# A graph network's setup rearranged: where the adjacency flags go, when signs are checked, which engine takes the first norms, and when later weights load

## The chip, the cores and the metric

The kernel runs on one core of a Trainium2 chip. The time is that of one execution on the device, in microseconds. Lower is better. Three executions of the kernel before took 4068.27, 4077.92 and 4077.22 us; their median is 4077.22 us.

The core has five instruction queues that work beside each other: TensorE (PE in the profile; its weight loads are listed apart as PEld), VectorE (DVE), ScalarE (ACT), GpSimd (POOL) and SyncE (SP), which here issues nearly all DMAs. Each queue runs its instructions in the order in which they stand in the program and waits on semaphores for the others.

## What is computed

The input is x, 16 graphs of 1024 nodes with 256 features each, and one adjacency matrix adj of 1024 x 1024 integers, shared by all graphs. Four layers follow, each of the form

```
h = max(layernorm(x), 0)
x = x + layer(h, adj)
```

Layers 0, 1 and 2 are graph attention: q = h W, a score for each pair of nodes from two dot products (leaky ReLU of their sum), masked where adj is not positive, a softmax over the neighbours, and the weighted sum of q, then ELU (layers 0 and 2) or ReLU (layer 1). Layer 0 has four heads of 64 features, layers 1 and 2 have one of 256. Layer 3 is a transformer block with eight heads of 32: queries, keys and values, scores masked by adj > 0, softmax, weighted sum, a residual with a layer norm, a feed-forward of two 256 x 256 products and another residual with a layer norm. All is in float32.

## The kernel before

`direct` computes everything with exponentials that are not shifted by their maximum, and at the end makes a flag that says whether that was safe; only if not, a slower function (`general`) runs after it. Part of the safety check is that adj has no negative entry: `least` holds the minimum of each row of adj.

**Tiling.** A graph's x is two half tiles `xh` of 128 partitions x 4 x 256 (1024 nodes are 8 blocks of 128). The mask is one tile of bytes, 128 x 8 x 1024, adj transposed, made once and kept. `w_aug[l]` holds the weights W of graph layer l with three columns per head added, which give the two dot products.

**Setup** (`setup`). `prepare(l)` loads W and the vector a of layer l, and VectorE multiplies and sums them into the added columns (L585, L596, L606, L614). `neighbours(it)`, for each of the eight row blocks of adj, loads 512 KB into a tile of the ring `pa` (L623); VectorE turns it into flags 0 or 1 in a second tile of `pa` (L628); TensorE transposes them (L531), ScalarE casts the result to bytes in the mask (L646), and VectorE takes the minimum of the integers (L655). The ring `pa` has six tiles, so that three blocks of adj can be in work at once. Then come the weights of layer 3.

**The start of a graph** (`begin`). x[b] is loaded in two halves (L1600); ScalarE sums each block (L1610) and its squared deviations (`spread_of`, L444 and L448); in `gat`, VectorE and GpSimd turn these into 1/standard deviation (`inverse_of_squares`, L460 and L468), and ScalarE applies the norm (`normal`, L502).

**A graph layer** (`gat`). TensorE transposes the normed blocks and multiplies them with `w_aug` (L772); ScalarE takes exponentials of the added columns (L783). The row side of the exponentials is transposed, written to DRAM (`turn_rows`, L845) and read back to all partitions (`spread`, L854) as `row`. VectorE makes the masked attention weights `pt` from `row`, a column and the mask (`weights`, L870). Layer 0 multiplies them in four column groups of TensorE (L984, and L994 for the sums), layers 1 and 2 in full form (L897).

**Layer 3** (`attention`). Queries and keys are projected (L1134), split into two parts `hi` and `lo` whose sum is exact, written to DRAM (`hl`, L1152) and copied back into the stacks `ks` and `qs` (L1158), so that one matmul (L1355) gives a score of full precision. ScalarE takes the exponential (L1379), VectorE applies the mask (L1388), and TensorE multiplies with the values in four column groups (L1220). `feed` does the feed-forward; its `back` loads x again in four parts (L1505) and stores the result (L1577).

**What sets the order.** Nothing of this is emitted where it stands in the code. Each step is recorded with its engine, an estimated duration, what it reads and writes, and a key; a key comes from a base (the graph's number) and a curve over the layer's steps (`KNOTS`). `Record.schedule` then plays the steps forward with these durations, gives each engine the ready step of the lowest key, and emits them in that order. `PASS` is the delay that it counts from an engine's end to a reader on another engine, `SLACK` the same for DMAs; `moved` and `lands` are a DMA's time on the engines and to its landing; `LEAD` moves ScalarE's and VectorE's keys forward; `BIAS` weighs TensorE's cost of changing between its forms (`SWITCH`). So a changed constant can move any instruction of the kernel. Buffers are rings: a new use waits for the last readers of the old one. While graph 0 is in layer 0, graph 1 goes through layer 0 beside it with buffers lent by layer 3 (`lent`).

Of the kernel before, what the change touches and what calls it, by code (L numbers as in the profile page):

```python
# [22 lines left out]
P = 128  # L23
# [93 lines left out]
PASS = {"pe": 0.122, "act": 0.556, "dve": 0.232, "pool": 0.13, "dma": 0.0}  # L117
# [26 lines left out]
class Record:  # L144
# [138 lines left out]
SLACK = 0.722  # L283
KNOTS = {
    "gat0": (-10.926, -10.742, -7.218, -4.626, -2.628, -2.099, -0.444, -3.636, -2.816),
    "gat1": (0.191, 0.25, 0.454, 0.45, 0.566, 0.582, 0.633, 1.016, 0.672),
    "gat2": (1.126, -0.076, -0.221, -0.062, 0.894, -0.428, 0.959, 1.018, 1.17),
    "beside": (1.093, 3.374, 4.836, 2.176, 5.971),
    "values": (1.444, -1.53, -3.682, -3.253, 0.902, 0.891, 2.874, 0.851, 0.421),
    "steps": (0.98, 1.188, 1.323, 1.512, 1.578, 1.712, 2.006, 2.02, 1.489),  # L290
    "feed": (2.026, 2.163, 1.768, 1.658, 2.343, 1.828, 2.009, 2.223, 3.042),
    "last": (3.521, -0.495, 0.103, 1.329, 1.339, 5.969, 5.585, 3.41, 5.439),
}
BIAS = 2.241
LEAD = {"act": 8.212, "dve": 0.635}
# [33 lines left out]
def direct(ctx, tc, flag, x, adj, gat_w, gat_a, w_qkv, ln1_g, ln1_b, ln2_g, ln2_b, w1, b1, w2, b2, out):  # L329
# [219 lines left out]
    b_aug = [Buf(t, []) for t in w_aug]  # L549
    b_mask, b_least, b_qkv, b_feed = (Buf(t, []) for t in (mask, least, wqkv_sb, w1_sb))  # L550

    def prepare(l):
# [11 lines left out]
            [],  # L564
# [11 lines left out]
            [],  # L576
# [42 lines left out]
    def neighbours(it):  # L619
        a32, nat = r_pa.new(), r_pa.new()  # L620
# [4 lines left out]
        nat_f = nat.t.rearrange("p a n -> p (a n)")  # L625
        dve(
            ts_us(N),
            lambda: nc.vector.tensor_scalar(nat_f, a_i, 0.0, None, ALU.is_gt),  # L628
            [nat],
            [a32],  # L630
        )
        for j0 in range(0, NT, TH):
# [9 lines left out]
                [nat],  # L642
# [10 lines left out]
        dve(  # L653
            tt_us(N),
            lambda: nc.vector.tensor_reduce(least[:, it : it + 1], a_i, AX.X, ALU.min),  # L655
            [b_least(it)],
            [a32],
        )

    def mask_of(hf):  # L660
        return [b_mask((it, j0)) for it in range(hf * TH, (hf + 1) * TH) for j0 in (0, TH)]

    def setup():
        rec.stream(-3.0, (0.0, 1.0), False)
        prepare(0)
        rec.stream(-0.9, (0.0, 0.1), False)
        for it in range(NT):
            neighbours(it)
# [8 lines left out]
            [],  # L677
# [10 lines left out]
        dma(5.0, 2.5, load_feed, [b_feed], [], us=5.7)  # L688
# [38 lines left out]
    def gat(xt, b_mv, b_rstd, l, my):  # L727
# [8 lines left out]
        for hf in range(2):  # L736
# [3 lines left out]
            inv = inverse_of_squares if l in SQUARED else inverse  # L740
# [107 lines left out]
        def spread(hf, h, rd):  # L848

            row = my.row.new()  # L850
            dma(
                1.2,
                2.07,
                lambda: nc.sync.dma_start(  # L854
                    row.t,
                    rd.t[h * TH : (h + 1) * TH, :]
                    .rearrange("t n -> (t n)")
                    .partition_broadcast(P),
                ),
                [row],  # L860
                [rd],
            )
            return row
# [220 lines left out]
    def attention(b, xt, b_mv, b_rstd):  # L1084
# [42 lines left out]
        def project(g, hf, keys, stack, at):  # L1127
# [23 lines left out]
            for k, part in enumerate((hi, lo)):  # L1151
                dma(0.65, 1.5, lambda: nc.sync.dma_start(hl.t[:, k, :], part.t), [hl(k)], [part])  # L1152
            for a in range(4):
                k = ((0, 0, 1, 1), (0, 1, 0, 1))[keys][a]
                dma(
                    1.0,
                    1.83,
# [77 lines left out]
        for n in range(len(steps) + LAG):  # L1235
            m = n - LAG
            if m >= 0:
# [13 lines left out]
                elif jt % run:  # L1251
                    for ss, pt in zip(sums[g, hf], pas[m]):
                        dma(
                            2.8,
                            0.85,
# [145 lines left out]
    def feed(b, x3, hn):  # L1401
# [95 lines left out]
        def back(hf):  # L1497
            yT = yTs[hf]
            for it in (hf * TH, hf * TH + 2):
# [3 lines left out]
                    1.0,  # L1503
                    1.83,
# [86 lines left out]
    def begin(b):  # L1591
        xt, b_mv, b_rstd = Halves(r_xh), r_mv.new(), r_rstd.new()
        x_b = x[b].rearrange("(t p) c -> p t c", p=P)
        rec.stream(b, (0.0, 0.0), False)
        for hf in range(2):
# [6 lines left out]
                [],  # L1602
                b - 1.0,
            )
        for hf in range(2):
            its = range(hf * TH, (hf + 1) * TH)
            for it in its:
# [18 lines left out]
    def graph(b, state, l, my=own, knots=None):  # L1626
        rec.stream(b, knots or KNOTS[f"gat{l}"])
        gat(*state, l, my)
# [17 lines left out]
    states = [begin(0), begin(1)]  # L1646
    graph(0, states[0], 0)
    borrowed = lent()
    graph(0, states[1], 0, borrowed, KNOTS["beside"])
    for r in vars(borrowed).values():  # L1650
        if isinstance(r, Lent):
            r.give_back()
    for b in range(NB):
# [617 lines left out]
```

## Time and profile before

| | us |
|---|---|
| median of three executions | 4077.22 |
| the profiled execution, whole | 4072.03 |
| its span (first to last instruction) | 4070.3 |
| busy: TensorE | 4012.3 |
| busy: VectorE | 3501.7 |
| busy: ScalarE | 2666.6 |
| busy: GpSimd | 621.0 |

A busy TensorE is not TensorE at its peak: matmuls overlap, and their ends are modelled. The profile also has the clock that was granted to TensorE: 0.50 to 1.00 in the first 60 us, 1.00 nearly all the time after that. In the rows of the profile, the arrow in brackets names what ended the idle time before an instruction. The chain of waits follows the work back from the last instruction: at each step to what released it, or to the instruction before it on its engine.

### The profile page before, as it was taken

To read this page: it belongs to the slowest core of one execution; us is meant where nothing else is said; L and a number is where in the kernel's file an instruction comes from. 1 tells how busy PE (TensorE), PEld (TensorE's weight loads), DVE (VectorE), ACT (ScalarE), POOL (GpSimd) and SP (SyncE) were. 2 spreads that over 40 slices of the span, in tenths; PEclk is the share of its full clock that TensorE was granted. 3 is DMA by queue.
4 is the path that set the end of the run, shared out by engine and by line. 5 is a ranking of instruction groups with operands and counts; after the bars stand their busy time and mean duration, and the time that the engine had idled before them with its cause. 6 is when DMAs were issued, how large, how long until landed. Compare 5 with 4: busy or idle time off the path is not lost.

```text
span 4070.3 us, 66071 instructions
## 1 busy us (share of the span) xinstructions
PE 4012.3 (99%) x23874; PEld 2352.0 (58%) x23874; DVE 3501.7 (86%) x5994; ACT 2666.6 (66%) x6673; POOL 621.0 (15%) x631
## 2 busy tenths in 40 slices
PE   7999999999999999999999999999999999999998
PEld 4566466564655646566564665646556465665643
DVE  7778898989989899898988989899898998989866
ACT  5467575775757767576675766757577675766765
POOL 1101111111111112111111111111111121111200
PEclk9999999999999999999999999999999999999999
DMA  3034454444545345463444544445543454624451
GB/s 128 27 103 115 126 126 109 113 104 115 124 125 123 83 117 126 115 150 76 126 110 123 127 110 113 104 115 122 127 121 82 117 128 115 150 69 121 112 137 51
DMA packets 227520, 456.54 MB, mean 112 GB/s; under 512 B 24688, under 2 KB 59760, under 8 KB 227184
## 3 DMA queue, kind: packets, MB, share of 16 engines
q1 hardware_dynamic: 192624, 326.39, 28.3%
q0 software_dynamic: 34560, 125.84, 16.2%
q8 instruction: 190, 3.11, 0.3%
q14 instruction: 146, 1.20, 0.1%
HBM read 225.25 MB, written 101.06 MB: 80 GB/s over the span
## 4 chain that ended last, share of the span: by engine, by line
PE 94%; DMA 3%; ACT 1%; DVE 1%; issue 0%; SPq 0%; DVEq 0%; ACTq 0%; POOLq 0%
PE bank L897 21%; PE bank L1220 16%; PE sc L1355 12%; PE bank L984 11%; PE bank L772 9%; PE bank L531 6%; PE sc L1134 5%; PE bank L1452 5%; PE bank L994 5%; PE sc L1172 3%; DMA sums<-pa 2%; PE sc L531 1%; DVE pt L870 1%; ACT waste L448 0%; ACT pa L1379 0%
## 5 line engine op out<-in xcount | busy, mean ns | idle before, releaser
L1388 DVE TENSOR_TENSOR pa<-pa,mask 128x1024 f32<-128x1024 f32 x1024 | 1222.7, 1219 | 166.1 <-ACT pa L1379 162.6
L1379 ACT ACTIVATE pa<-sc 128x512 f32<-128x512 f32 x2048 | 1101.6, 611 | 370.1 <-DVE sums L1247 174.4
L870 DVE SCALAR_TENSOR_TENSOR pt<-row,e,mask 128x512 f32<-128x512 f32 x1472 | 1011.9, 744 | 46.6 <-DMA row<-rd 27.7
L897 PE MATMUL bank<-qb,pt 128*128 128x257 f32 x4096 | 941.0, 380 | 0.0
L897 PEld LDWEIGHTS bank<-qb,pt 128*128 128x128 f32 x4096 | 770.6, 190 | 143.6 <-issue 20.1
L1355 PE MATMUL sc<-qs,ks 128*128 128x512 f32 x2048 | 727.9, 457 | 2.6 <-DMA hl<-hi 1.1
L1220 PE MATMUL bank<-pa,va 128*32 128x512 f32 x4096 | 515.0, 597 | 0.0
L1355 PEld LDWEIGHTS sc<-qs,ks 128*128 128x128 f32 x2048 | 361.3, 189 | 237.9 <-ACT pa L1379 82.5
L984 PE MATMUL bank<-pt,qb 128*32 128x512 f32 x3840 | 461.7, 596 | 6.5 <-DVE pt L870 6.5
L1247 DVE TENSOR_TENSOR sums<-pa,pa 128x1024 f32<-128x1024 f32 x360 | 434.1, 1220 | 16.7 <-PE bank L1220 14.2
L772 PE MATMUL bank<-w_aug,hT 128*128 128x259 f32 (+1 forms) x1504 | 373.3, 389 | 0.0
L1256 POOL DMA_DIRECT2D sums<-pa x240 | 211.5, 883 | 954.1 <-DVE pa L1388 426.6
L772 PEld LDWEIGHTS bank<-w_aug,hT 128*128 128x128 f32 x1504 | 280.3, 190 | 99.6 <-ACT qb L794 35.4
L925 ACT ACTIVATE ex<-bank,rec 128x256 f32<-128x256 f32 x256 | 121.4, 475 | 288.9 <-DVE rec L917 288.7
L984 PEld LDWEIGHTS bank<-pt,qb 128*32 128x32 f32 x3840 | 116.5, 110 | 294.8 <-issue 219.5
L1220 PEld LDWEIGHTS bank<-pa,va 128*32 128x32 f32 x4096 | 115.0, 109 | 250.6 <-issue 225.7
L994 PE MATMUL bank<-pt,e 128*32 128x512 f32 x1920 | 252.0, 593 | 0.1
L1134 PE MATMUL sc<-hTa,wqkv_sb 128*128 128x512 f32 x512 | 240.0, 596 | 0.0
L468 POOL TENSOR_TENSOR rstd<-rstd,neg_half 128x4 f32<-128x4 f32 x96 | 169.2, 1762 | 362.1 <-DVE rstd L460 362.0
L1143 ACT CAST hi<-sc 128x512 fp32r<-128x512 f32 x128 | 75.1, 587 | 211.8 <-PE sc L1134 122.0
L502 ACT ACTIVATE hn<-xh,mv,rstd 128x256 f32<-128x256 f32 x376 | 202.8, 613 | 7.5 <-DVE mv L492 4.1
L1220 PE MATMUL bank<-sums,ones 128*32 128x512 f32 x1440 | 200.5, 600 | 3.9 <-DMA sums<-pa 3.7
(152 smaller groups left out, 4501.0 us busy)
## 6 DMA issues: line engine op xcount, KB each, us to landing
sums<-pa POOLq DMA_DIRECT2D x240, 512.0 KB, 6.0
ks<-hl SPq DMA_DIRECT2D x256, 256.0 KB
qs<-hl SPq DMA_DIRECT2D x256, 256.0 KB
row<-rd SPq DMA_DIRECT2D x184, 256.0 KB
hl<-hi SPq DMA_DIRECT2D x128, 256.0 KB
hl<-lo SPq DMA_DIRECT2D x128, 256.0 KB
xh<-in_x_dram SPq DMA_DIRECT2D x32, 512.0 KB
x<-xh SPq DMA_DIRECT2D x32, 512.0 KB
```

The costliest lines, as they stand in the source:

```text
L531: nc.tensor.transpose(dst(k), src(k), ident[:shape, :shape])
L772: nc.tensor.matmul(g.t[:, : C + 3 * H], hT.t[:, ct, k * P : (k + 1) * P], w_aug[l][:, ct, :], start=ct == 0, stop=ct == CT - 1,)
L870: lambda: nc.vector.scalar_tensor_tensor(pt.t, row.t, e3[:, 2, jt // TH, h, jt % TH : jt % TH + 1], mask[:, jt, hf * HALF : (hf + 1) * HAL ...
L897: nc.tensor.matmul(g.t[:, : D + 1], pts[jt].t[:, k * P : (k + 1) * P], qb[:, jt, 0, :], start=jt == 0, stop=jt == NT - 1,)
L984: nc.tensor.matmul(g.t[u * D + d : u * D + d + D3, :], qb[:, j, h + u, d : d + D3], pts[u][j - jt].t, start=j == 0, stop=j == NT - 1,)
L994: nc.tensor.matmul(gd.t[c : c + D3, :], one(jt + k, h + u).to_broadcast([P, D3]), pts[u][k].t, start=jt == 0, stop=jt == NT - 2,)
L1134: nc.tensor.matmul(sc.t, wqkv_sb[:, ct, c0 : c0 + P], hT.t[:, ct, hf * HALF : (hf + 1) * HALF], start=ct == 0, stop=ct == CT - 1,)
L1220: nc.tensor.matmul(ac.t[r * D3 : (r + 1) * D3, :], columns(r), of_head(r), start=first, stop=last,)
L1247: lambda: nc.vector.tensor_add(ss.t, p0.t, p1.t),
L1355: nc.tensor.matmul(scs[r - r0].t, ks.t[:, r, jt * P : (jt + 1) * P].bitcast(F32R), q.t[:, r, :].bitcast(F32R), start=True, stop=True,)
L1379: lambda: nc.scalar.activation(pt.t[:, v, :], sc.t, AF.Exp, scale=1.0 / math.sqrt(D3)),
L1388: lambda: nc.vector.tensor_mul(pt.t, pt.t, mask[:, jt : jt + 1, i0 : i0 + HALF].to_broadcast([P, 2, HALF]),),
```

## The change

Five things are edited.

1. The flags of the adjacency blocks go into the key stack `ks`, which nothing uses before layer 3, and no longer into tiles of `pa`. It has four parts of 128 x 1024, so that four blocks of flags are in work, and up to six loads of adj.
2. The minimum for the sign check is taken out of `neighbours`. A new function `signs`, recorded after graph 0's and graph 1's layer 0, loads adj a second time into the two tiles `yT` of the feed-forward and takes the minimum there.
3. Graph 0's first norm takes mean and variance from VectorE (`stats`: bn_stats and bn_aggr, L437 and L438, then `inverse`, L480 and L492), where ScalarE made sums and squares. The other graphs stay as they were.
4. Later loads are made to wait for the reads of the first rows in `spread`: x of graph 1 for the second, x of graph 2 and the weights of graph layers 1 and 2 for the fourth, the weights of layer 3 for the eighth. These are waits for the row's landing (`AFTER_ROWS`), ahead of the load on SP's queue.
5. The planner's constants: `PASS`, `SLACK`, `KNOTS`, `BIAS`, `LEAD`, and `moved` and `lands` of several DMAs have new values.

```diff
-PASS = {"pe": 0.122, "act": 0.556, "dve": 0.232, "pool": 0.13, "dma": 0.0}
+PASS = {"pe": 0.05, "act": 0.5, "dve": 0.263, "pool": 0.13, "dma": 0.0}
...
-SLACK = 0.722
+SLACK = 0.71
 KNOTS = {
...
-BIAS = 2.241
-LEAD = {"act": 8.212, "dve": 0.635}
+BIAS = 1.386
+LEAD = {"act": 10.373, "dve": 1.021}
...
+    rows_out = Buf(None, [])
+    n_rows = [0]
+    AFTER_ROWS = [[rows_out(n)] for n in range(8)]
...
 prepare(l): loads of w_aug and a
-            [],
+            AFTER_ROWS[3] * (l > 0),
...
-    def neighbours(it):
-        a32, nat = r_pa.new(), r_pa.new()
+    def neighbours(it, nat):
+        a32, part = r_pa.new(), nat(it % HG)
...
-        nat_f = nat.t.rearrange("p a n -> p (a n)")
+        nat_f = nat.t[:, it % HG, :]
         dve(
             ts_us(N),
-            lambda: nc.vector.tensor_scalar(nat_f, a_i, 0.0, None, ALU.is_gt),
-            [nat],
+            lambda: nc.vector.tensor_scalar(nat_f.bitcast(F32R), a_i, 0.0, None, ALU.is_gt),
+            [part],
...
-        dve(
-            tt_us(N),
-            lambda: nc.vector.tensor_reduce(least[:, it : it + 1], a_i, AX.X, ALU.min),
-            [b_least(it)],
-            [a32],
-        )
+
+    def signs():
+        rec.stream(0, (0.9, 1.6), False)
+        for it in range(NT):
+            again = r_yT.new()
+            a_i = again.t.rearrange("p a n -> p (a n)").bitcast(I32)
+            dma(1.8, 1.7, lambda: nc.sync.dma_start(a_i, adj[it * P : (it + 1) * P, :]), [again], [])
+            dve(
+                tt_us(N),
+                lambda: nc.vector.tensor_reduce(least[:, it : it + 1], a_i, AX.X, ALU.min),
+                [b_least(it)],
+                [again],
+            )
...
 setup
+        nat = r_ks.new()
         for it in range(NT):
-            neighbours(it)
+            neighbours(it, nat)
+
+    def setup_later():
         rec.stream(-0.5, (0.0, 0.3), False)
         prepare(1)
         prepare(2)
 loads of w_qkv and of the feed-forward's weights
-            [],
+            AFTER_ROWS[7],
...
 spread
-                1.2,
-                2.07,
+                1.45,
+                1.75,
...
-                [row],
+                [row] + [rows_out(n_rows[0])] * (n_rows[0] < 8),
                 [rd],
             )
+            n_rows[0] += 1
...
 begin
-        rec.stream(b, (0.0, 0.0), False)
+        rec.stream(b, (0.0, 0.0) if b else (-5.0, -5.0), False)
...
-                [],
+                AFTER_ROWS[1 if b == 1 else 3] * (b in (1, 2)),
                 b - 1.0,
             )
         for hf in range(2):
             its = range(hf * TH, (hf + 1) * TH)
+            if b == 0:
+                for it in its:
+                    stats(xt.at(it), xt(it), b_mv.t[:, 0, it, :], b_mv((0, it)))
+                continue
...
     setup()
-    states = [begin(0), begin(1)]
-    graph(0, states[0], 0)
+    states = [begin(0)]
+    graph(0, states[0], 0, first=True)
+    setup_later()
+    states.append(begin(1))
     borrowed = lent()
     graph(0, states[1], 0, borrowed, KNOTS["beside"])
     for r in vars(borrowed).values():
         if isinstance(r, Lent):
             r.give_back()
+    signs()
```

## The prediction

> **What bounds the kernel now.** I read the page first (span, busy shares, chain), then the first 60 us in windows of 20 us, the order of time in that stretch, the chain of waits row by row, and last the stretch where TensorE stops near the end.
>
> ```profile
> span 4070.3 us, 66071 instructions
> PE 4012.3 (99%) x23874; PEld 2352.0 (58%) x23874; DVE 3501.7 (86%) x5994; ACT 2666.6 (66%) x6673; POOL 621.0 (15%) x631
> ...
> PE 94%; DMA 3%; ACT 1%; DVE 1%; issue 0%; SPq 0%; DVEq 0%; ACTq 0%; POOLq 0%
> ```
>
> TensorE is the bound: only 58 us of the span are free of it. A change can win those 58 us, the stretches in which TensorE runs slowly, or the cost of changing between its instruction forms; elsewhere nothing.
>
> ```profile
> 0.00:20.00 20.00, 4.78 (x25) 4.32 (x26) 12.84 (x35) 13.02 (x39) 1.89 (x8) 0.96 0.86 313
> 20.00:40.00 20.00, 16.45 (x90) 14.36 (x89) 15.34 (x37) 15.46 (x48) 1.58 (x3) 0.84 0.77 229
> 40.00:60.00 20.00, 14.92 (x100) 5.34 (x100) 12.19 (x25) 17.92 (x62) 4.91 (x4) 0.77 0.09 28
> 60.00:80.00 20.00, 19.60 (x150) 9.56 (x147) 18.38 (x34) 7.52 (x17) 0.75 (x1) 1.00 0.10 27
> 80.00:100.00 20.00, 19.61 (x158) 7.67 (x160) 19.96 (x43) 6.09 (x15) 2.91 (x2) 1.00 0.19 55
> ```
>
> Columns: window, length, busy us of PE, PEld, DVE, ACT, POOL, clock, DMA share, GB/s. TensorE idles 15.2 + 3.6 + 5.1 = 24 us in the first 60. From 60 on it is full, but VectorE is as full (18.4 and 20.0 of 20). At 40 to 60 ScalarE is the full one (17.9).
>
> ```profile
> 10.50 0.69 DVE L628 TENSOR_SCALAR pa<-pa 128x1024 f32<-128x1024 int32 x1 [1.91 <-DMA pa<-in_adj_dram]
> 30.23 0.34 SPq L845 DMA_DIRECT2D rd<-rt  x1
> 34.41 0.82 SPq L854 DMA_DIRECT2D row<-rd  x2
> 43.14 0.17 DVE L460 TENSOR_SCALAR rstd<-mv 128x4 f32<-128x4 f32 x1 [5.35 <-ACT waste L448]
> 43.21 5.38 DVE L870 SCALAR_TENSOR_TENSOR pt<-row,e,mask 128x512 f32<-128x512 f32 x8
> 44.10 4.01 PE L984 MATMUL bank<-pt,qb 128*32 128x512 f32 x14 [6.51 <-DVE pt L870]
> 51.99 0.17 DVE L460 TENSOR_SCALAR rstd<-mv 128x4 f32<-128x4 f32 x1 [1.86 <-ACT waste L448]
> ```
>
> The first weights (L870) start at 43.2: VectorE stands 5.35 us in an L460 that needs batch 1's squares (L448) from ScalarE, which is busy with batches 1 and 2. It stands there again at 52. The row write took 4.2 us from its issue at 30.23 to the row read at 34.41, while other loads kept the DMA engines 0.77 to 0.86 busy.
>
> **Setup.** Removed from ScalarE: batch 0's eight sums (0.54 us a step at L1610), eight squares (0.64 at L448) and two L444 (0.2): 9.8 us. Added to VectorE: eight bn_stats and bn_aggr; four pairs took 1.6 us at 83.5 to 85.8 in the trace, so 3.3. Removed from early VectorE: eight sign reductions of 1.21 (L655), 9.7 us. In the new order eight bn_stats stand ahead of the first flags, so the first flags come not at 10.5 but at: x lands 7.7 (first L1610), plus 3.3, plus the w_aug work between (1.6) = about 12.9. TensorE so starts at 13.6 where it started at 11.3, which costs 2.3. After that the flags need no buffer turn-round: six adjacency loads are out at once instead of three, and the flags have the key stack's four places to themselves. The two x half loads come first as before. ScalarE does four norms (0.52) from 12.2, four mask casts (0.6), two copies, four norms, four casts: to 24. The projections (four of 0.9) follow their banks to 26, their second half to about 32; the first row write goes at 28.5 and, with the other loads held back, its read at about 31 (2.2 instead of 4.2 us). First weights at about 35, first L984 at about 36 instead of 44.1: **-8**. The L460 waits after it (TensorE's slow stretch from 44 to 52, about 5 us beyond its matmuls at later rates) go, because batch 1's x is asked for only after the second row, and its L460 stands behind sixteen weights (10.6 us): **-5**. What is late next is VectorE: the w_aug work for layers 1 and 2 (16 of 0.42, 8 of 0.16: 8 us; before it stood in VectorE's waits) now falls among the weights at 60 to 115 us, where VectorE has no room but TensorE has layer 1's matmuls soon after. Between 0 and 8 of it reach TensorE; I take **+5**, since 80 to 100 is 19.96 of 20. Setup -8, bounds -13 and 0. On F32R flags no row of VectorE exists: 0.69 each (L628) if nothing changes, 1.21 (the full-rate L655) if it does, so 0 to 4.2 us; I take 0, the row nearest in operation.
>
> The granted clock belongs here: 0.50 at 20 to 25 and 40 to 45, each after TensorE had idled (16.0 to 19.8, 37.6 to 44.1); 16 L531 took 3.66 us early against 0.89 for 8 later. The Trainium skill (TensorE: Matmul & The Clock Gate, Part 1) says that an idle window of about 3.4 us halves the clock and that one busy window restores it. By that rule a start without such gaps would regain about 5 us of half-speed work. I count none of it by itself; most of it is inside the 5 above.
>
> **Held loads on SP's queue.** x of batch 1 waits for row 2's landing, x of batch 2 and w_aug for row 4, w_qkv and the feed weights for row 8. Behind them stand the next row reads, which wait for a free row buffer anyway (two buffers; SP waited 73 times for L870 weights). Cost 0; if that cover went, a landing of 3 us each time, three times, in a DVE-full stretch: +9 at most.
>
> **Signs later.** Eight 512 KB loads into two tiles and eight 1.21 reductions move to the turn from batch 0's graphs to its attention. VectorE has room there: 7.8 of 20 busy at 160 to 180, 22.4 of 50 at 200 to 250. But six loads wait on SP for the reduction before, with hl, ks and qs behind. A 256 KB reload took 2.85 us in the chain, so a turn is about 4 us; all six on the path would be +24, none 0. The planner put two or three between projections whose results are needed at once; I take **+3**.
>
> **The order of everything else.** The planner's constants and curves change, so TensorE's order changes all along; its instructions do not. What an order costs is read from the chain:
>
> ```profile
> 114.25 0.86 PE bank L994 x8
> 115.11 1.02 PE bank L531 x8
> 116.14 1.85 PE bank L984 x16
> 117.99 0.86 PE bank L994 x8
> 118.85 1.95 PE bank L772 x8
> ```
>
> Eight L772 take 1.82 after their own kind and 1.95 here, sixteen L984 1.72 and 1.85: a turn into four-column form (L984, L994, L1220) and out again costs 0.26. A visit to the scores (L1355) from full form costs about 0.06: in the order of time four scores start at 1013.00 and the next form at 1014.01, 1.01 us, where four take 0.92 in the chain at 3918; four L531 ahead of them start at 1012.59 and last 0.41 instead of 0.44. Counted in the two built orders, column visits fall from 413 to 397, score visits from 736 to 667: 16 x 0.26 + 69 x 0.06 = **-8**. Bounds -2 (score visits free, half the column price) and -12 (direction of each change priced apart).
>
> **The last batch.** No later batch fills TensorE there:
>
> ```profile
> 3892.30 0.39 SPq L1577 DMA_DIRECT2D out_dram<-xr  x1
> 3897.55 0.32 SPq L1505 DMA_DIRECT2D xr<-x  x1
> 3897.99 0.39 SPq L1577 DMA_DIRECT2D out_dram<-xr  x1
> 3901.47 0.32 SPq L1505 DMA_DIRECT2D xr<-x  x1
> 3901.89 1.81 SPq L1158 DMA_DIRECT2D qs<-hl  x4
> ```
>
> The first queries' copies stand behind two stores and two reloads until 3901.9, though their data was written at 3891.5; scores start at 3911.2, and TensorE loses about 14 us by 3920. In the new order these copies stand ahead of the stores; only the second half of the keys, wanted four steps later, is behind one. The copies go 8 us sooner: **-8**, bounds -12 and 0 (norms at L502 hold TensorE 4.9 us in the same place).
>
> **Sum.** -8 +3 -8 -8 = -21. Against the profiled execution's own 4072.0 (span 4070.3): 4051. The median of the runs shown is 4077.2, from 4068.3 to 4077.9; the profiled one lies in the lower half, so I put 2 on it: 4053. Under 0.3% (12.2 us on 4077.2) this kernel's runs can't tell a change.
>
> **Rivals.**
> 1. Gains swallowed, 0.2. VectorE is the real bound to 115 us: the w_aug work costs all 8, flags at 1.21 add 4: setup 0. Switches -2, last batch -4, signs +3: 4069, within 0.3%. For it: 19.96 of 20. Against it: layer 1's matmuls need little VectorE (7.8 of 20 at 160). That the start is not sooner at all is this case.
> 2. Slower, 0.12. The planner now counts 0.05 us from TensorE to a reader (was 0.122) and 0.5 from ScalarE (was 0.556). Queues run in their written order, so if the old figures were the true ones, each of 1,024 score pairs can wait for its bank. At 0.05 a pair: +51, 4102. It decides from 0.035 a pair (36 us: the 21 and 12 more, with the profile's 3 to 5 below the median). Against it: TensorE waits for L1379 at the scores only 0.7 us in all now.
> 3. Better than forecast, 0.08: setup -13, switches -12, last batch -12, signs 0: 4035.
>
> The forecast has 0.6; its own range is 4038 to 4064. The range of all, 4036 to 4086, leaves out rival 2's bulk and the end of rival 3. Faster: 0.6 + 0.08 + a little of rival 1 = 0.71; same 0.17; slower 0.12.
>
> **What would show it.** Right: first L984 at 34 to 38; no L460 waiting 5 us for L448; clock 1.00 from 26 on; DVE over 19 of 20 through 110; no TensorE gap over 3 us in the last batch's first scores; PE busy below 4000. Wrong: first L984 after 42; SP waiting in L667 with PE idle at 215 to 330; PE rows at L1378 idling behind L1402; a new gap where the last batch's second keys are read.

## The result and the profile after

The kernel after took 4060.06 us (median of 7 runs, 4056.57 to 4066.36), the kernel before 4072.20 us beside it (7 runs, 4068.26 to 4077.92). The ratio is 0.9971, 95% interval 0.996 to 0.9982: faster by 12 us, just at the 0.3% that the prediction took as the limit of what can be told. 4053 was predicted, 4036 to 4086 as the range; 0.71 was put on faster.

The page of the kernel after, its first lines and the shares of the chain of waits:

```profile
span 4064.5 us, 65781 instructions
PE 4005.3 (99%) x23874; PEld 2354.6 (58%) x23874; DVE 3495.1 (86%) x6010; ACT 2691.8 (66%) x6639; POOL 640.0 (16%) x631
...
PE 80%; DMA 6%; ACT 5%; DVE 4%; issue 3%; POOL 1%; SPq 0%; POOLq 0%; DVEq 0%; ACTq 0%
```

The profiled execution of the kernel after (4066.36 us, the longest of its seven) is 5.7 us shorter than that of before; which stages are shorter still in the median run no profile shows. TensorE is busy 7.0 us less and idle 1.2 us more (59.2 for 58.0). So the idle time, of which the prediction meant to take some 13 us (its sum without the turns), did not shrink at all in this execution. Where it went is seen when both runs are cut at the same places. First before, then after; columns: window, length, busy us of PE, PEld, DVE, ACT, POOL, clock, DMA share, GB/s.

```profile
0.00:50.00 50.00, 27.12 (x144) 21.17 (x148) 34.41 (x83) 38.09 (x122) 5.93 (x13) 0.83 0.66 217
50.00:121.00 71.00, 69.16 (x556) 27.73 (x549) 63.49 (x121) 26.44 (x68) 6.76 (x6) 1.00 0.13 38
...
300.00:3880.00 3580.00, 3575.31 (x21294) 2114.91 (x21293) 3158.27 (x5360) 2391.42 (x5990) 579.47 (x581) 1.00 0.47 116
3880.00:3925.00 45.00, 37.00 (x141) 20.56 (x140) 17.00 (x38) 21.59 (x51) 5.01 (x6) 0.85 0.62 155
```

```profile
0.00:50.00 50.00, 33.94 (x230) 22.00 (x234) 31.67 (x81) 29.61 (x80) 5.22 (x12) 0.99 0.52 182
50.00:121.00 71.00, 64.05 (x487) 27.06 (x480) 61.47 (x137) 30.73 (x84) 7.51 (x8) 0.98 0.21 63
...
300.00:3880.00 3580.00, 3564.07 (x21271) 2120.51 (x21270) 3146.59 (x5362) 2414.36 (x5962) 591.02 (x575) 1.00 0.47 115
3880.00:3925.00 45.00, 44.83 (x207) 25.89 (x207) 24.29 (x51) 32.66 (x80) 6.00 (x8) 1.00 0.82 207
```

Length less PE busy is TensorE's idle time (differences are taken before rounding):

| window, us | before | after | |
|---|---|---|---|
| 0 to 50 | 22.9 | 16.1 | -6.8 |
| 50 to 121 | 1.8 | 7.0 | +5.1 |
| 121 to 300 | 1.4 | 2.0 | +0.6 |
| 300 to 3880 | 4.7 | 15.9 | +11.2 |
| 3880 to 3925 | 8.0 | 0.2 | -7.8 |
| 3925 to the end | 19.2 | 18.1 | -1.1 |

The start (first L1007 10.6 us sooner than the first L984 of before) and the last batch's idle time gave about what was forecast. The stretch right behind the start took most of its gain back, and the long middle took 11 us that no term of the sum had.

Idle time is not all. TensorE also runs slowly for a while after a gap. In the last batch of before the granted clock was 0.50 from 3899.4 to 3902.8 and from 3906.2 to 3916.5 us:

```profile
3900.00:3910.00 10.00, 5.02 (x14) 3.00 (x13) 1.54 (x4) 2.91 (x6) 1.02 (x1) 0.67 0.71 175
3910.00:3920.00 10.00, 9.36 (x27) 4.63 (x29) 2.36 (x2) 5.66 (x11) 0.00 (x0) 0.68 0.54 134
```

TensorE worked 11.4 us at this half clock there, and none in the kernel after. Counted as half lost, that is 5.7 us on top of the 7.8 of idle time: the last batch gave some 13.5 us. Up to 3880 us the kernel after has 40.9 us idle where before has 30.8, and as much work at half clock (10.2 and 10.5 us). So by these counts it is some 10 us behind up to there, and in this execution what comes after 3880 us, the last batch above all, puts it ahead.

The start of the kernel after, in order of time:

```profile
12.31 0.69 DVE L632 TENSOR_SCALAR ks<-pa 128x1024 fp32r<-128x1024 int32 x1
28.50 0.81 SPq L876 DMA_DIRECT2D row<-rd  x2
31.75 10.92 DVE L893 SCALAR_TENSOR_TENSOR pt<-row,e,mask 128x512 f32<-128x512 f32 x16 [0.18 <-DMA row<-rd]
33.54 2.48 PE L1007 MATMUL bank<-pt,qb 128*32 128x512 f32 x14
43.76 0.17 DVE L460 TENSOR_SCALAR rstd<-mv 128x4 f32<-128x4 f32 x1 [1.08 <-ACT waste L448]
53.46 1.41 DVE L893 SCALAR_TENSOR_TENSOR pt<-row,e,mask 128x512 f32<-128x512 f32 x2 [2.08 <-PE bank L1017]
62.02 2.08 DVE L893 SCALAR_TENSOR_TENSOR pt<-row,e,mask 128x512 f32<-128x512 f32 x3 [1.89 <-DMA row<-rd]
66.62 1.17 PE L794 MATMUL bank<-w_aug,hTa 128*128 128x268 f32 x4 [1.45 <-DVE rec L1063]
87.89 0.28 PE L860 MATMUL bank<-ident,xr 128*16 128x128 f32 x1 [1.39 <-DVE rec L1063]
```

(L632 makes the flags, L628 of before; L870 is L893 now, L984 is L1007, L994 is L1017, L854 is L876, L1379 is L1402, L1355 is L1378, L1220 is L1243, L1388 is L1411.) The first weights start at 31.75 instead of 43.2, the first L1007 at 33.54 instead of 44.1, and the wait of 5.35 us for L448 is 1.08. Then the waits pass from one queue to the next: VectorE for TensorE, for a row, TensorE for VectorE's L1063, which stands behind weights. Each is 1 to 2 us.

TensorE's waits from 121 to 3880 us (engine, what it waited to run, for what: us in total, times, longest), before and then after:

```profile
PE bank L1220 <- DMA sums<-pa: 3.7, 7, 1.5
PE sc L1355 <- DMA hl<-hi: 1.1, 1, 1.1
PE sc L1355 <- ACT pa L1379: 0.7, 1, 0.7
```

```profile
PE sc L1378 <- ACT pa L1402: 9.5, 12, 2.0
PE bank L920 <- DVE pt L893: 5.9, 14, 0.4
PE sc L1378 <- DMA rd<-rt: 1.5, 1, 1.5
```

Once in nearly every batch (one graph's work) a score pair waits for ScalarE to empty its bank, and a full-form product of layers 1 and 2 for its weights (both come about 248 us apart, the length of a batch). Before had the first once, for 0.7 us, and the second not at all. In the last batch, the gap of before is gone:

```profile
3900.26 1.74 SPq L1181 DMA_DIRECT2D qs<-hl  x4
3902.19 0.17 DVE L480 TENSOR_SCALAR rstd<-mv 128x4 f32<-128x4 f32 x1
3903.49 0.16 DVE L492 SCALAR_TENSOR_TENSOR mv<-mv,rstd 128x4 f32<-128x4 f32 x1 [1.13 <-POOL rstd L483]
3909.41 1.17 PE L1378 MATMUL sc<-qs,ks 128*128 128x512 f32 x4
```

The queries' copies go ahead of the stores (3907.5 and 3910.5 in this trace), and L480 and L492 follow each other with only GpSimd's step between them.

### The profile page after: what moved, and what is told of

It reads as the page before. It is cut to its first block, busy times and chain, and to the rows that moved or that the text cites. A ratio compares the mean times of both kernels' runs of the same rounds, so it can differ in the third digit from the quotient of the medians.

```text
span 4064.5 us, 65781 instructions
## 1 busy us (share of the span) xinstructions
PE 4005.3 (99%) x23874; PEld 2354.6 (58%) x23874; DVE 3495.1 (86%) x6010; ACT 2691.8 (66%) x6639; POOL 640.0 (16%) x631
## 4 chain that ended last, share of the span: by engine, by line
PE 80%; DMA 6%; ACT 5%; DVE 4%; issue 3%; POOL 1%; SPq 0%; POOLq 0%; DVEq 0%; ACTq 0%
PE bank L920 18%; PE bank L1243 13%; PE bank L1007 10%; PE sc L1378 9%; PE bank L794 7%; PE bank L1475 5%; PE bank L531 5%; PE bank L1017 5%; DMA sums<-pa 5%; PE sc L1157 4%; PE sc L1195 2%; DVE pt L893 2%; ACT pa L1402 2%; POOL sum_e L844 1%; ACT hn L502 1%
## 5 line engine op out<-in xcount | busy, mean ns | idle before, releaser
L1411 DVE TENSOR_TENSOR pa<-pa,mask 128x1024 f32<-128x1024 f32 x1024 | 1217.7, 1215 | 85.8 <-ACT pa L1402 84.1
L1402 ACT ACTIVATE pa<-sc 128x512 f32<-128x512 f32 x2048 | 1089.5, 601 | 294.8 <-PE sc L1378 164.4
L893 DVE SCALAR_TENSOR_TENSOR pt<-row,e,mask 128x512 f32<-128x512 f32 x1472 | 1016.4, 742 | 48.6 <-DMA row<-rd 36.4
L1378 PE MATMUL sc<-qs,ks 128*128 128x512 f32 x2048 | 715.8, 456 | 10.9 <-ACT pa L1402 9.5
L1243 PE MATMUL bank<-pa,va 128*32 128x512 f32 x4096 | 520.2, 598 | 1.2 <-DVE pa L1411 1.1
L1378 PEld LDWEIGHTS sc<-qs,ks 128*128 128x128 f32 x2048 | 364.8, 188 | 243.8 <-ACT pa L1402 80.0
L1007 PE MATMUL bank<-pt,qb 128*32 128x512 f32 x3840 | 462.1, 596 | 0.3 <-DVE pt L893 0.3
L1007 PEld LDWEIGHTS bank<-pt,qb 128*32 128x32 f32 x3840 | 117.4, 110 | 280.9 <-issue 218.3
L1243 PEld LDWEIGHTS bank<-pa,va 128*32 128x32 f32 x4096 | 118.2, 109 | 256.8 <-issue 226.0
L1017 PE MATMUL bank<-pt,e 128*32 128x512 f32 x1920 | 252.8, 592 | 0.0
L502 ACT ACTIVATE hn<-xh,mv,rstd 128x256 f32<-128x256 f32 x376 | 194.9, 594 | 28.9 <-DVE mv L492 27.6
L1038 ACT COPY ot<-bank 128x512 f32<-128x512 f32 x120 | 70.1, 586 | 213.5 <-PE bank L1007 196.6
L1243 PE MATMUL bank<-sums,ones 128*32 128x512 f32 x1440 | 201.4, 602 | 0.5 <-DMA sums<-pa 0.5
L844 POOL TENSOR_TENSOR sum_e<-sum_e,e 128x12 f32<-128x12 f32 (+1 forms) x94 | 95.1, 1012 | 671.7 <-ACT e L805 671.3
```

The costliest lines, as they stand in the source:

```text
L502: lambda: nc.scalar.activation(dst, src, func, bias=bias, scale=scale),
L893: lambda: nc.vector.scalar_tensor_tensor(pt.t, row.t, e3[:, 2, jt // TH, h, jt % TH : jt % TH + 1], mask[:, jt, hf * HALF : (hf + 1) * HAL ...
L1007: nc.tensor.matmul(g.t[u * D + d : u * D + d + D3, :], qb[:, j, h + u, d : d + D3], pts[u][j - jt].t, start=j == 0, stop=j == NT - 1,)
L1017: nc.tensor.matmul(gd.t[c : c + D3, :], one(jt + k, h + u).to_broadcast([P, D3]), pts[u][k].t, start=jt == 0, stop=jt == NT - 2,)
L1243: nc.tensor.matmul(ac.t[r * D3 : (r + 1) * D3, :], columns(r), of_head(r), start=first, stop=last,)
L1378: nc.tensor.matmul(scs[r - r0].t, ks.t[:, r, jt * P : (jt + 1) * P].bitcast(F32R), q.t[:, r, :].bitcast(F32R), start=True, stop=True,)
```

## The experiments

Ratios are against runs of the kernel before on the same chip in the same session; 0.001 is 4.1 us. "Order held" means that the order is planned as in the kernel named, and only the steps mentioned are then moved or left out. The lead at 121 us, which the expectations speak of, is how much more of the program's matmul time TensorE has done by then than in the kernel before (each kind of matmul priced alike in all traces; the prices are fitted, so it is an estimate, good to 1 or 2 us).

| kernel | ratio | 95% interval |
|---|---|---|
| after | 0.9971 | 0.996 to 0.9982 |
| const_only | 1.0022 | 1.0013 to 1.0031 |
| setup_only | 1.0064 | 1.0052 to 1.0076 |
| queries_first | 1.0008 | 1.0 to 1.0017 |
| norms_first | 1.0009 | 1.0 to 1.0018 |
| norms_queries | 0.999 | 0.998 to 0.9999 |
| no_signs | 0.9967 | 0.9954 to 0.998 |
| late_graph2 | 0.9963 | 0.995 to 0.9976 |
| no_columns | 0.9965 | 0.9952 to 0.9978 |
| undo_hold | 1.0009 | 1.0 to 1.0019 |
| undo_norms | 0.9971 | 0.9959 to 0.9982 |
| old_pass | 1.037 | 1.0352 to 1.0387 |
| pass_0505 | 1.0238 | 1.0221 to 1.0255 |

### The two halves of the change apart

const_only is the kernel before with the new planner's constants; setup_only is the kernel after with the old ones.

```diff
 const_only, on the kernel before
-PASS = {"pe": 0.122, "act": 0.556, "dve": 0.232, "pool": 0.13, "dma": 0.0}
+PASS = {"pe": 0.05, "act": 0.5, "dve": 0.263, "pool": 0.13, "dma": 0.0}
 ... and SLACK, KNOTS, BIAS, LEAD and the times of five DMAs
 setup_only, on the kernel after: the same lines the other way round
```

> The setup of before, all planner constants of the change. First theory: the change's gain of 12 us comes from the order that the constants make (fewer turns of TensorE between forms, the first queries of the last batch ahead of the stores), and the setup nets 2 us or less. Then this kernel is at 0.9973 of before (4061 on 4072), TensorE starts L984 at about 44 us, and the last batch has no gap over 3 us. Rival: the setup's 10 us at the first product last to the end, and the order's savings are spent again in waits in the middle; then this kernel is within 3 us of before.

> All of the rearranged setup, planner constants of before; the turns of TensorE (412 column visits, 733 score visits) and the SP order in the last batch are those of before. First theory: 0 to 4 us under before (4068 to 4072), first L1007 near 34 us, and most of the lead gone by 120 us; the gap of 12 us in the last batch is there. Rival: 10 to 12 us under before (4060 to 4062).

Both miss. Each half alone makes the kernel slower, by 9 and by 26 us, and only both together make it faster, by 12. The windows of const_only (columns as above) show two of the changes in the table, and from where they come:

```profile
0.00:50.00 50.00, 28.19 (x154) 19.60 (x158) 33.57 (x82) 38.90 (x125) 6.06 (x13) 0.90 0.64 217
...
300.00:3880.00 3580.00, 3562.49 (x21220) 2111.23 (x21221) 3138.30 (x5339) 2409.43 (x5941) 591.80 (x575) 1.00 0.47 115
3880.00:3925.00 45.00, 44.84 (x225) 28.74 (x224) 25.54 (x62) 36.86 (x94) 8.83 (x11) 1.00 0.71 173
```

With the old setup, the new constants close the last batch's gap (0.2 us idle) and bring the middle's waits (17.5), just as in the kernel after. The waits there are of the same kind and as many as in the kernel after (12 for ScalarE's exponential, 14 for weights). So these two belong to the constants, and the shorter start to the setup's edits. setup_only keeps the start (15.2 us idle to 50 us). It too has 16.3 us idle in the middle, but 13.4 of them stand before 1000 us and do not come back in each batch. The last batch's gap is still there (7.1 us of waiting for L502, now behind 3925, where TensorE idles 29.1 us), and TensorE is busy 8.5 us longer than before. Why neither half works without the other is not shown; that each set of curves suits the setup it came with is a guess.

### The last batch

queries_first takes up the prediction's cause of the gap; norms_first and norms_queries a second one, found in the trace of before: on VectorE, two additions (L1511) that wait for reloads of xr surround L480 and L492, the norm for which the transposes L531 wait 4.9 us. All three have the order of before held.

```diff
 queries_first: the four copies qs<-hl of the last batch's first queries
+        order[at:at] = first      # right behind the write that they read, ahead of two stores
 norms_first: the two additions xr += c2 around that norm
+        order[at:at] = residual   # right behind L492
 norms_queries: both
```

> Before, its order held everywhere but for one thing: in the last batch the four copies of the first queries stand on SP's queue ahead of the two stores and two reloads. The prediction's step gives -8, bounds -12 and 0. If the SP queue is the cause of the 14 us lost at 3895 to 3920: 4060 to 4064, ratio 0.997 to 0.998, first L1355 of that batch about 8 us sooner. Rival: the norms at L502 and the landing hold TensorE anyway; ratio over 0.9993.

> The kernel before, its order held, with two additions of VectorE (L1511, xr plus c2, in the last stretch) moved behind the two steps of the feed-forward's norm (L480, L492) that they surrounded. Theory of two locks: the gap of 15 us at 3895 to 3920 is closed by two things, the norm that stands behind additions which wait for reloads (to 3906.9), and the first queries' copies that stand behind the same reloads on SP's queue (to 3901.9, landed at about 3911). With the norm free alone the transposes L531 move from 3907.8 to about 3902, but the first scores still start at 3911, so the time changes by 0 to -2 us. Theory of the norm alone: scores at 3905 to 3906, -5 to -6 us. Rival, that neither is the cause: transposes still after 3907, 0 us.

> The kernel before, its order held, with both edits of the last stretch: the two additions behind the norm's steps, and the four copies of the first queries ahead of the stores on SP's queue. Theory of two locks: first scores at 3903 to 3905 where they started at 3911, the idle time of TensorE from 3895 to 3920 down from about 15 to 7 us, -6 to -9 us in all. Theory of the norm alone: the same as with the norm's edit alone. Rival, that neither is the cause (the keys' or the queries' landing, or ScalarE): 0 to -1 us.

TensorE's waits from 3885 to 3925 us, in before, queries_first, norms_first and norms_queries in this order (in the last three, L504 is L502 of before, L533 is L531, L1357 is L1355, L1226 is L1220 and L1394 is L1388; a wait of 2.4 us for L1146 is the same in all four and is left out):

```profile
PE bank L531 <- ACT xh L502: 4.9, 1, 4.9
PE sc L1355 <- DMA qs<-hl: 0.6, 1, 0.6
```

```profile
PE bank L533 <- ACT xh L504: 9.5, 1, 9.5
```

```profile
PE sc L1357 <- DMA qs<-hl: 5.2, 1, 5.2
PE bank L533 <- ACT xh L504: 1.2, 1, 1.2
```

```profile
PE bank L1226 <- DVE pa L1394: 1.5, 1, 1.5
PE bank L533 <- ACT xh L504: 1.2, 1, 1.2
```

With the copies first, the reloads come later and the norm with them: 9.5 us in place of 5.5. With the norm first, TensorE waits 5.2 us for the copies. Only both together open the gap. From the transposes of ota to the first scores it is 17.1 us in before (3894.06 to 3911.20), 20.6 in queries_first, 16.9 in norms_first and 11.5 in norms_queries. The times follow: no gain from either alone, and about 4 us (interval 0 to 8) from both, where 6 to 9 were expected. The window from 3880 to 3925 still has 5.2 us idle, and 5.6 us of work at half clock where before has 11.4. (The loss of 14 or 15 us that the prediction and the expectations put here is therefore not all idle time: 8.0 us are, and the rest is work at half clock.) So the theory of two locks held in kind, with a smaller gain than it gave, and that of one cause did not, whichever cause is taken.

### The sign check

no_signs is the kernel after, order held, without the eight second loads of adj and their minima; it doesn't check the signs.

```diff
         for w in rec.schedule():
-            w.emit()
+            if w.tag != "signs":
+                w.emit()
```

> The changed kernel with its order held, but the eight second loads of adj and the eight minimum reductions left out (the minimum is taken as 0, so the check of adj's sign is missing). The prediction put the moved sign check at +3 (0 to 24). If so, 3 us under the changed kernel, 4057, and the 5 us that TensorE loses between 240 and 260 us shrink. Rival: it is hidden: within 1 us of the changed kernel, 4060.

0.9967 against 0.9971, intervals nearly the same: the later loads and minima cost nothing that can be measured. TensorE's waits from 200 to 330 us are 2.0 us in the kernel after, the longest of them for rd, and 1.3 without the signs.

### Who takes the start's lead

After 50 us the kernel after has a lead of some 10 us, at 121 us 2. Two suspects were taken away one at a time, with the order of after held.

```diff
 late_graph2: graph 2's sums and squares on ScalarE
+    one behind every fourth step of ScalarE from layer 1 of graph 0 on, not in the first 90 us
 no_columns: VectorE's steps of prepare(1) and prepare(2)
+    left out; the columns are zero
```

> The kernel after, its order held, except that ScalarE's 16 sums and squares of graph 2 (L1633, L444, L448 as they stood) are taken out of the first 90 us and spread behind the first layer-1 work of graph 0. Theory that ScalarE eats the lead of the start: the changed kernel is 10 to 12 us ahead of the one before at 34 to 50 us and 2 ahead at 121; ScalarE is busy 16.0 of 20 us from 40 to 60 with the statistics of graphs 1 and 2. Then the lead at 121 is 5 to 9 us and the time 3 to 7 us below that of the kernel after (ratio to before 0.9955 to 0.9965 where after has 0.997). Theory that VectorE's columns eat it: no more than 1 us less. Rival, that anything gained before 121 us is lost again to waits later: ahead at 121, and the same time.

> The kernel after, its order held, without VectorE's work on the added columns of layers 1 and 2 (24 instructions, 8 us); these columns are zero, so what this kernel computes is not the reference. Theory of the prediction (columns among the weights cost 0 to 8 us, 5 taken): the lead at 121 us goes from 2 to 5 to 8 us and the time is 3 to 6 us below that of the kernel after. Theory that ScalarE eats the lead: at most 1 to 2 us. Rival, that what is won before 121 us is lost in later waits: ahead at 121, same time.

They gain some 3 and 2 us on the kernel after, less than the intervals can tell. The lead at 121 us is 4.0 in late_graph2 and 2.9 in no_columns. That is no more than one execution differs from another: from 0 to 121 us TensorE idles 23.0 us in the kernel after, 21.4 in late_graph2, 22.7 in no_columns, and 22.6 in no_signs, which in this stretch is the kernel after. From 50 to 121 us it idles 6.5 and 7.5 us; it was 7.0. The wait for L1063 (L1069 in no_columns) stays, with 8 us of VectorE's work gone:

```profile
87.21 0.28 PE L866 MATMUL bank<-ident,xr 128*16 128x128 f32 x1 [2.35 <-DVE rec L1069]
```

So neither of the two alone takes most of the lead. By the waits shown above it is the order in which VectorE's steps stand: L1063 waits behind weights, these for a row or for a tile of `pt` that TensorE still reads. This is read from the trace; no run moved L1063 alone. Undoing two of the edits measures what the lead is worth:

```diff
 undo_hold, on the kernel after
-    AFTER_ROWS = [[rows_out(n)] for n in range(8)]
+    AFTER_ROWS = [[] for n in range(8)]
 undo_norms, on the kernel after
-            if b == 0:
-                for it in its:
-                    stats(xt.at(it), xt(it), b_mv.t[:, 0, it, :], b_mv((0, it)))
-                continue
...
-        gat(*state, l, my, l in SQUARED and not first)
+        gat(*state, l, my, l in SQUARED)
```

> The kernel after with all later loads free again (the list of waits for the rows is empty; the planner orders again, 392 column visits and 666 score visits against 397 and 667). Theory of the prediction: while x of graph 1 and 2 and the weights load, the first row's write and read take about 4 us instead of 1.4 to 2.2, so the first weights start 2 to 4 us later than the 31.75 of the kernel after (at 34 to 36), and TensorE has lost 2 to 4 us more at 34 us. Rival, that the row read is fast for another reason (fewer loads in flight by then anyway): first weights within 1 us of 31.75. For the time: if what is won before 50 us melts until 121 us, it stays within 3 us of the kernel after (4058 to 4064); if it doesn't melt, +2 to +4.

> The kernel after with graph 0's first norm back on ScalarE's sums and squares (the planner orders again; column, score and full visits of TensorE are the same 397, 667 and 706). Theory of the prediction: ScalarE has 9.8 us more ahead of the first norms, VectorE 3.3 less, so TensorE's flags start about 2 us sooner (11.3) but the first weights and the first L1007 some 4 to 7 us later than 31.75 and 33.54. Rival, that the flags' transposes set the first weights: within 1 us. For the time: within 3 us of the kernel after if the start's lead melts anyway by 121 us, +4 to +7 if not.

In order of time, undo_hold and then undo_norms:

```profile
27.77 2.38 SPq L1623 DMA_DIRECT2D xh<-in_x_dram  x4
30.25 0.45 SPq L876 DMA_DIRECT2D row<-rd  x1
38.44 5.39 DVE L893 SCALAR_TENSOR_TENSOR pt<-row,e,mask 128x512 f32<-128x512 f32 x8 [6.58 <-DMA row<-rd]
39.34 3.94 PE L1007 MATMUL bank<-pt,qb 128*32 128x512 f32 x14 [5.44 <-DVE pt L893]
```

```profile
33.97 0.81 SPq L876 DMA_DIRECT2D row<-rd  x2
37.11 5.39 DVE L893 SCALAR_TENSOR_TENSOR pt<-row,e,mask 128x512 f32<-128x512 f32 x8 [1.13 <-DMA row<-rd]
```

Without the hold, the row read stands behind four loads of x and takes 8.2 us to the first weights (30.25 to 38.44), where it takes 3.25 in the kernel after: 6.7 us later, twice what was expected. With the norms back on ScalarE the first weights are 5.4 us later, as expected. And that is not seen in the time: undo_norms has the same TensorE turns as the kernel after (397 column visits, 667 score visits) and the same ratio, 0.9971. Some 3 us of it are still there at 121 us (26.1 us idle until then for 23.0); the two intervals leave room for a loss of some 6. undo_hold is slower by some 15 us than the kernel after, but only about 1 us of its lag is there at 121 us; it has 9.6 us idle from 121 to 300, where the kernel after has 2.0, and at 300 us it is some 16 us behind. From 300 on both have the same order and wait alike (14.7 us for 15.9). So the loss lies between 121 and 300 us, which the planner orders differently; which of its choices costs this was not traced.

### The planner's delays and the turns

Both are the kernel after with one line of constants changed.

```diff
 old_pass
-PASS = {"pe": 0.05, "act": 0.5, "dve": 0.263, "pool": 0.13, "dma": 0.0}
+PASS = {"pe": 0.122, "act": 0.556, "dve": 0.232, "pool": 0.13, "dma": 0.0}
 pass_0505
-PASS = {"pe": 0.05, "act": 0.5, "dve": 0.263, "pool": 0.13, "dma": 0.0}
+PASS = {"pe": 0.05, "act": 0.505, "dve": 0.263, "pool": 0.13, "dma": 0.0}
```

> The kernel after with the old delays from engine to engine alone in the planner (0.122, 0.556, 0.232 us); the planner orders again: 513 column visits and 655 score visits against 397 and 667. Theory that the short delays make TensorE wait (score pairs for the exponentials of the bank before, L1378 for L1402, 9.5 us in the kernel after): these waits fall under 3 us, and the time is the turns' 116 x 0.26 = 30 us minus 7 to 15, so +15 to +23 on the kernel after, 4075 to 4083. Theory that turns count as in the prediction and the delays don't: +30, 4090, with waits as before. Rival, that turns cost much less than 0.26 (hidden where VectorE is late anyway): at or below the kernel after.

> The kernel after with one constant of the planner moved by one part in a hundred: the delay from ScalarE 0.505 instead of 0.5 us. The planner orders again: 548 column visits and 710 score visits against 397 and 667. Theory that the order's turns are what counts, at the prediction's prices: 151 x 0.26 + 43 x 0.06 = 42 us more work on TensorE, and with the same waits 4090 to 4105. Theory that the size of the delays counts and not the order they happen to give: 0 to +5 us. Rival, that turns are cheaper than priced because they lie in waits: +5 to +20.

Every theory misses by a wide margin: 3.7% and 2.4% slower than before, some 163 and 109 us over the kernel after. Waits of TensorE from 121 to 3880 us, in old_pass and in pass_0505, and of the latter the window of the middle:

```profile
PE bank L1243 <- DVE pa L1411: 32.5, 41, 1.3
...
PE sc L1378 <- ACT pa L1402: 4.1, 20, 0.3
```

```profile
PE sc L1157 <- ACT pa L1402: 21.1, 28, 1.0
PE bank L1475 <- DVE rec L1063: 10.8, 13, 0.9
```

```profile
300.00:3880.00 3580.00, 3526.49 (x20734) 2039.08 (x20734) 3067.70 (x5208) 2345.72 (x5781) 511.72 (x560) 1.00 0.47 112
```

The old delays do halve the wait that they were to cure (L1378 for L1402, 9.5 to 4.1), and bring 32.5 us of another one. A change of 0.005 us in one constant turns 397 column visits into 548 and has 53.5 us idle in the middle where the kernel after has 15.9; the rest of the loss is TensorE's busy time, 70 us more, where the turns by the prediction's prices are 42. A wait that comes 13 times is one place in the order, repeated about every 255 us in nearly each of the 16 batches; 28 times are two such places.

One number could have told this beforehand. `Record.schedule` keeps the end of the order that it plays forward in `self.end`, and this needs no run on the chip. Against before, in us:

| kernel | the planner's own end | its difference | measured (from the ratio) |
|---|---|---|---|
| before | 4063.2 | | |
| after | 4048.8 | -14 | -12 |
| const_only | 4065.5 | +2 | +9 |
| setup_only | 4083.6 | +20 | +26 |
| undo_hold | 4067.4 | +4 | +4 |
| undo_norms | 4054.1 | -9 | -12 |
| old_pass | 4226.1 | +163 | +151 |
| pass_0505 | 4172.8 | +110 | +97 |

Each sign is right and none is off by more than 13 us, though the delays that it counts with differ from row to row. Neither the prediction nor the expectations used it.

## Why the prediction was right, and where it was not

The time, the sign and the range held; 4060 lies inside the forecast's own 4038 to 4064. The sum did not: -21 was forecast, and the medians give -12. That the sum comes near is in part luck: setup and turns gave less than forecast and the middle lost 11 us, the last batch gave more. Of the signs that were to show it right, several did not come: PE busy was 4005.3 and not below 4000, the clock was 0.50 again at 48.9 to 52.3, VectorE was 17.0 and 15.7 of 20 at 60 to 100 and not over 19, and a sign of being wrong, L1378 behind L1402, did come. By its steps:

- **Setup, first weights, -8.** Right in kind, and a little small: TensorE starts at 13.15 (13.6 forecast), the row read goes at 28.50 (31), weights at 31.75 (35), L1007 at 33.54 (36). (The prediction's own sum for the first flags, 7.7 + 3.3 + 1.6, is 12.6 and not 12.9; they came at 12.31.) The flags with F32R output take 0.69 us as before, so this unknown cost 0. The term of the held loads was mis-sized: 2 us were put on the faster row, undo_hold shows 6.7.
- **The L460 waits, -5, and the columns, +5.** The waits fell from 8.3 to 2.0 us between 31 and 121. But what is late next was named wrongly. The added columns cost about 1 us by the lead at 121 us (no_columns; 2 us by its time, which the intervals cannot tell from 0 or 5), not 5; what came instead is the chain of small waits between rows, weights and L1063.
- **Setup in all, -8.** This step failed. Idle time to 121 us fell by 1.7 only, the lead at 121 us is 2, and in undo_norms 5 us at the first weights are 3 at 121 us and not seen in the time. The prediction carried most of an early saving of 10 us to the end of the kernel. Its first rival (setup 0, at 0.2) had the size, but not the reason: the start was sooner, and VectorE was not full right behind it (17.0 and 15.7 of 20 from 60 to 100 us).
- **Held loads on SP, 0, and signs, +3.** No cost of the first is seen. The second is nothing that can be measured (no_signs: 2 us less, with intervals of some 5; 0.7 us less idle time from 121 to 300).
- **Turns, -8.** This step failed too. TensorE's busy time fell by 7.0 us, but that is the clock: over the whole span, TensorE worked 23.6 us at half clock in before and 10.4 in after, and half of the difference is 6.6 us. With half of this work taken off, the busy times are 4000.5 and 4000.1 us. Other executions of these two orders lie between 4000 and 4005 us by the same count, so the 16 column and 69 score visits that are gone saved nothing that can be seen. const_only, with 8 column and 63 score visits fewer than before (6 us by the same prices), has 0.6 us more busy time than before.
- **The last batch, -8.** The idle time was right in size (-7.8), the cause half of it, and the half clock behind the gap was left out: 11.4 us of work that now run at full clock, worth 5.7 us more. Both the SP queue and the norms that the prediction mentioned as a bound held the same gap, and either alone gives nothing.
- **What was missing: +11 in the middle.** The prediction counted what the new order saves and not what it makes wait. Its second rival had the mechanism (L1378 for L1402 was to show it) with a price for all 1,024 pairs; it came at 12 of them. That the smaller delays cause it fell with old_pass: what decides is how the whole order happens to fit, and the size of a single constant doesn't tell. The planner's own end had it.

So the forecast was 7 us too low: setup and turns were overrated, and the middle was left out. The rivals' times (4069, 4102, 4035) lack the 2 us that the forecast adds for the median; it changes nothing here. The flags' move alone was not tried.

## What to carry to other kernels

Where a planner with fitted constants writes the order, a change of the program and a change of the constants can't be priced apart: here each alone lost, and 1% of one constant cost 2.7% of the kernel after. Read the planner's own end first; it had all seven differences within 13 us, and the count of turns had not. Then look for each step that has moved ahead of its data, because waits that recur once a batch can weigh more than the setup. A saving at the start counts only as far as the order behind it lets it through, and a gap costs its idle time and the half clock behind it. A gap that several queues hold is closed only when all of them let go.

## What was not expected of the hardware

- The clock halves without a long idle stretch. The windows of the kernel after:

```profile
45.00:46.00 1.00, 0.51 (x8) 0.00 (x0) 0.94 (x3) 0.97 (x5) 0.02 (x1) 1.00 1.00 263
...
49.00:50.00 1.00, 1.00 (x9) 0.27 (x12) 1.00 (x4) 0.97 (x5) 0.00 (x0) 0.50 0.98 322
```

TensorE was busy some 2.7 of the 4 us from 45 to 49, with no single gap over 0.8, and then ran at 0.50 until 52.3: sixteen L1007 took 3.50 us from 49.07 and 1.89 from 53.26. The stretches at half clock last 3.41, 6.83 or 10.24 us in the traces of before and after (but for the one at the end of each), which fits a clock that is set anew every 3.41 us. In the 3.41 us that end at the kernel after's drops (48.9, 250.3 and 806.7 us) TensorE was busy 2.15, 2.02 and 1.67 us. The Trainium skill (TensorE: Matmul & The Clock Gate, Part 1) puts half clock behind an idle window of about 3.4 us and full clock behind a busy one. The first is too narrow for this case: a window that is half to two thirds busy can be enough. It need not be: from 110.3 to 113.7 us TensorE was busy 1.83 of 3.41 us and kept the full clock. The second agrees: in before, work began again at 44.1, the window from 42.3 to 45.7 was 1.64 us busy and did not bring the clock back, and the one from 45.7 to 49.15 was busy throughout and did.

- The same order does not wait alike in each execution. Idle time from 300 to 3880 us was 4.7, 4.7, 7.2 and 9.3 us in the four kernels that have the order of before there (before, queries_first, norms_first, norms_queries), and 14.4 to 16.8 in the six with that of after (after, undo_norms, undo_hold, no_signs, late_graph2, no_columns). A single profile tells these two orders apart, but not differences of 4 us. Part of the spread of the times goes with the clock: the seven runs of the kernel after took 4065.1 us on average at a mean granted clock of 0.997 (three runs), 4058.4 at 0.998 (three) and 4056.6 at 0.999 (one).
- A row read of 256 KB to all partitions behind four loads of x of 512 KB each took 8.2 us until its first reader started (undo_hold), and 3.25 with next to nothing ahead (after: DMA share 0.00 to 0.05 from 22 to 28.5 us).
